# Softmax of a window attention: subtraction and sum moved from six ScalarE instructions to VectorE, beside a long scan

## The chip, the cores and the metric

The kernel runs on one core of a Trainium2 chip. The metric is the device time of one execution in microseconds (us). The engines are named as in the profile: PE (TensorE; PEld are its weight loads), DVE (VectorE), ACT (ScalarE), POOL (GpSimd) and SP (SyncE, which issues most DMAs).

## The reference, cut to what matters

The network has four layers on images of 56 x 56 pixels and 192 channels, eight images. L0, L1 and L2 are state space layers: each runs a selective scan in four directions over all 3136 pixels. L0 has convolutions beside its scan. L3 is a window attention with an MLP. The change touches the softmax of L3 alone:

```python
qkv = xw @ qkv_w.T + qkv_b            # windows of 7 x 7 = 49 pixels, 6 heads
attn = einsum('bhnd,bhmd->bhnm', qn, kn) * scale
attn = attn + (14.0 * sigmoid(rpb))[None]
attn = attn + mask
attn = softmax(attn, axis=-1)         # exp(a - max a) / sum over 49 columns
out = einsum('bhnm,bhmd->bnhd', attn, v)
```

and the scan that runs beside it is, for each direction, channel and state:

```python
h = exp(d_t * A) * h + (d_t * u_t) * b_t
y = einsum('bkdn,bkn->bkd', h, c_t)
```

## The kernel before, in words

**The scan sets the order.** `run` (line 816) cuts the three scan layers of all eight images into units, and each unit into 24 steps, so that there are 9216 steps. One step handles 128 rows (32 channels by 4 states) and 784 pixels. For step s:

- `make` (line 1044) lets ACT write the decay `exp(A*delta)` into a PSUM tile `ps_x`, of which there are two buffers, and lets POOL write `db`, the product of the spread input and B, of which there are four.
- One step later DVE runs the scan over `ps_x` and `db` (line 888), in place in `ps_x`, and multiplies the result with C into `hc`. In every fourth step the scan writes to `hc` instead, and POOL makes the product there.
- Two steps later ACT copies the last column of the scan into `state` (line 876), for the next unit. In the program this copy stands ahead of the next decay on ACT.
- Four steps later PE sums the products of three steps into `ps_y`.

`prepare` (line 980) makes the step sizes of every half unit (12 steps): PE multiplies, ACT loads the softplus table, makes `delta` and loads the table of exp and ln again, POOL makes `du`, and DMAs spread both to 128 rows.

**Everything else is put between the steps.** The convolutions of L0, the norms and the attention of L3 are Python generators. After each step, `run` lets pieces of them go (line 913) for as long as the planned PE and ACT time of the step is not spent. `Meter` (line 92) books a planned cost for each instruction; what is booked for DVE and POOL holds nothing back. `yield 0` ends a piece within a step, `yield 1` asks for a later step. The order of instructions on every engine is thus fixed when the program is built. `in_order` (line 940) keeps it.

**The attention.** `attention_block` (line 1092) handles the image before the one being scanned: images 0 to 6 go beside the scans of the images after them, and image 7 comes when the scans are over, with `self.ending` set and eight PSUM banks instead of two. Each image has eight rows of windows and each row four calls of `pair` (line 1205), two of which run in turn. One call handles two windows: PE puts bias and scores of all six heads into one bank (128 rows by 6 x 49 = 294 columns), DVE takes the maxima `mx` (negated), the exponentials `s` and their sums `sm` are made, DVE inverts the sums, POOL scales `s`, PE transposes it, and so on to the values. There are 7 x 8 x 4 = 224 calls beside the scans and 32 in the ending.

Two forms of the softmax stand in the code. Beside the scans (lines 1244 to 1252) ACT makes six exponentials of 49 columns from the bank, each with a bias from `mx` and an accumulated sum. In the ending (lines 1235 to 1242) DVE adds `mx` to all 294 columns, ACT makes one exponential, and DVE sums.

Of the kernel before, what the change touches and what calls it, by code (L numbers as in the profile page):

```python
# [32 lines left out]
AF = mybir.ActivationFunctionType  # L33
ALU = mybir.AluOpType
AX = mybir.AxisListType
# [23 lines left out]
WT = WS * WS  # L59
BT = NW * WT  # L60
HEADS = 6
# [77 lines left out]
class Net:  # L139
# [1004 lines left out]
    def attention(self, x, wi, bias, wqkv, wpr, q1, q2, stored):  # L1144

        nc = self.nc
# [58 lines left out]
        def pair(w0):  # L1205


            s = q2.tile([128, HEADS, WT], F32, name="s")
            mx = q2.tile([128, HEADS], F32, name="mx")
            sm = q2.tile([128, HEADS], F32, name="sm")  # L1210
            held = yield from self.bank()
            p = held[:, : HEADS * WT]
            for d in range(2):
                nc.tensor.matmul(
                    p[64 * d : 64 * d + 64], self.ident[:WT, :64],
                    bias[:, int(w0 + d == NW - 1)].rearrange("n h m -> n (h m)"),
                    start=True, stop=False,
                )
            for h in range(HEADS):
                for d in range(2):  # L1220
                    at = (h * NW + w0 + d) * WT
                    n = min(64, 6 * BT - at)
                    nc.tensor.matmul(
                        p[64 * d : 64 * d + n, h * WT : (h + 1) * WT], qn[:, at : at + n],
                        win(kn[:, h // 3], w0 + d), start=False, stop=h == HEADS - 1,
                    )
                if h == 2:
                    yield 0
            yield LAG + 1
            nc.vector.reduce_max(  # L1230
                mx, p.rearrange("n (h m) -> n h m", h=HEADS), axis=AX.X, negate=True
            )
            yield 1
            if self.ending:
                nc.vector.tensor_add(
                    s, p.rearrange("n (h m) -> n h m", h=HEADS),
                    mx.unsqueeze(2).to_broadcast([128, HEADS, WT]),
                )
                self.free(held)
                nc.scalar.activation(s, s, AF.Exp)  # L1240
                yield 1
                nc.vector.reduce_sum(sm, s, axis=AX.X)
            else:
                for h in range(HEADS):
                    nc.scalar.activation(
                        s[:, h, :], p[:, h * WT : (h + 1) * WT], AF.Exp,
                        bias=mx[:, h : h + 1], accum_out=sm[:, h : h + 1],
                    )
                    if h % 2:
                        yield 0  # L1250
                self.free(held)
                yield 1
            nc.vector.reciprocal(sm, sm)
            held = yield from self.bank()
            p = held[:WT, : 2 * C].rearrange("n (d e) -> n d e", d=2)
            for d in range(2):
                w = w0 + d
                for c in range(2):
                    nc.tensor.matmul(
                        p[:, d], xw[:, c, w * WT : (w + 1) * WT], wqkv[:, c, 2 * C :],  # L1260
                        start=c == 0, stop=c == 1,
                    )
            nc.gpsimd.tensor_mul(s, s, sm.unsqueeze(2).to_broadcast([128, HEADS, WT]))
            yield LAG
            vt = q2.tile([WT, 2, C], F32, name="vt")
            self.copied(vt, p)
            self.free(held)
            pts = q2.tile([WT, HEADS, 2 * WT], F32, name="pt")
            both = self.ident.rearrange("p (d n) -> p d n", d=2)[:, :, :WT]
            for c in range(2):  # L1270
                held = yield from self.bank()
                p = held[:WT, : 6 * WT].rearrange("m (h d n) -> m h d n", h=3, d=2)
                for h in range(3):
                    nc.tensor.matmul(p[:, h], s[:, 3 * c + h, :], both, start=True, stop=True)
                yield LAG
                self.copied(
                    pts[:, 3 * c : 3 * c + 3, :], held[:WT, : 6 * WT].rearrange("m (h n) -> m h n", h=3)
                )
                self.free(held)
                yield 0  # L1280
            yield 1
            held = yield from self.bank()
            p = held[:CH, : 4 * WT].rearrange("e (c n) -> e c n", c=2)
            for c in range(2):
                for d in range(2):
                    for h in range(3):
                        g = 3 * c + h
                        nc.tensor.matmul(
                            p[HD * h : HD * h + HD, c, d * WT : (d + 1) * WT],
                            vt[:, d, HD * g : HD * g + HD], pts[:, g, d * WT : (d + 1) * WT],  # L1290
                            start=True, stop=True,
                        )
            yield LAG


            for c in range(2):
                nc.scalar.activation(
                    xw[:, c, w0 * WT : (w0 + 2) * WT], p[:, c], AF.Identity, bias=self.v("vb", c)
                )
            self.free(held)  # L1300

        yield from self.together(2, [pair(w) for w in range(0, NW, 2)])

        o = q1.tile([CH, 2, BT], F32, name="ao", tag="kn")
# [258 lines left out]
```

## Time and profile before

| what | us |
|---|---|
| median of three runs (26607.50 to 26614.08) | 26609.99 |
| the profiled execution, its own time | 26624.15 |
| its span in the profile | 26622.0 |
| first scan step to last scan step | 181 to 26060 |
| the ending (attention and MLP of the last image) | 26060 to 26622 |

| engine | busy us | share of the span | instructions |
|---|---|---|---|
| DVE | 24146.0 | 91% | 19164 |
| POOL | 23082.9 | 87% | 13255 |
| PE | 18403.8 | 69% | 76788 |
| ACT | 17059.2 | 64% | 30413 |

Nearly every instruction bears line 109, that of the `Meter` helper, so groups are told apart by their tiles: `ps_x<-dsp,A` is the decay, `ps_x<-ps_x,state,db` a scan, `s<-ps_p,mx` an exponential of the softmax beside the scans, `s<-s` one in the ending, `ps_p` and `ps_t` are PSUM banks. A group's row gives its count, its busy time, the mean of one in ns, and the idle time of the engine before it with what ended it. DVE's instructions overlap at their edges: the next one often starts some 80 ns ahead of the recorded end of the last.

### The profile page before, as it was taken

How to read it: one execution, taken by the hardware profiler on the slowest of the kernel's cores; microseconds unless marked ns; L12 is line 12 of the kernel's file. 1: busy time of each engine (PE TensorE's matmuls, PEld its weight loads, DVE VectorE, ACT ScalarE, POOL GpSimd, SP SyncE). 2: the span in 40 equal slices, each digit the busy share in tenths (PEclk: the TensorE clock that was granted, in tenths of full speed). 3: DMA queues.
4: the chain of work that ended last, by engine and by line, in shares of the span. 5: the costliest groups of instructions: out<-in, count | busy, mean ns of one | idle time of the engine just before them, and what ended most of it. 6: DMA issues, size and time to landing. Idle time of an engine off the chain costs nothing. (4 is left out here: it accounts for less than half of the span.)

```text
span 26622.0 us, 260231 instructions
## 1 busy us (share of the span) xinstructions
PE 18403.8 (69%) x76788; PEld 6418.9 (24%) x76788; DVE 24146.0 (91%) x19164; ACT 17059.2 (64%) x30413; POOL 23082.9 (87%) x13255
## 2 busy tenths in 40 slices
PE   6675567776676767767767676677766777677657
PEld 2221122222222222222222222222222222222214
DVE  5999999999999999998999999999899999999994
ACT  4655566666666656666666766667666676666654
POOL 5888988988889888898888988988888888889992
PEclk7776777777777777777777777777777777777767
DMA  4565565556555566555655556555565555655551
GB/s 95 136 140 121 133 138 135 131 128 140 138 133 131 129 140 137 133 130 129 143 134 135 131 130 143 133 131 129 132 142 132 133 129 135 139 133 134 130 131 41
DMA packets 1503447, 3472.21 MB, mean 130 GB/s; under 512 B 310618, under 2 KB 503219, under 8 KB 1502020
## 3 DMA queue, kind: packets, MB, share of 16 engines
q1 hardware_dynamic: 1496452, 3455.15, 56.7%
q8 instruction: 606, 9.93, 0.1%
q0 software_dynamic: 3072, 0.31, 0.1%
q14 instruction: 821, 6.73, 0.1%
q10 hardware_dynamic: 2496, 0.09, 0.0%
HBM read 1457.23 MB, written 147.89 MB: 60 GB/s over the span
## 5 line engine op out<-in xcount | busy, mean ns | idle before, releaser
L109 POOL TENSOR_TENSOR db<-usp,bt 128x784 f32<-128x784 f32 x9216 | 16851.6, 1857 | 118.6 <-DMA usp<-du 71.4
L109 DVE TENSOR_TENSOR_SCAN ps_x<-ps_x,state,db 128x784 f32<-128x784 f32 x5184 | 9564.9, 1845 | 623.1 <-ACT state L109 266.7
L109 ACT ACTIVATE ps_x<-dsp,A 128x784 f32<-128x784 f32 x9216 | 8444.0, 917 | 2515.6 <-DVE hc L109 2290.5
L109 PE MATMUL ps_y<-hc,esum 128*32 128x392 f32 x36864 | 6882.9, 639 | 1045.1 <-POOL hc L109 696.0
L109 DVE TENSOR_TENSOR hc<-ps_x,ct 128x784 f32<-128x784 f32 x6912 | 6736.8, 975 | 654.1 <-DVE ps_x L109 11.5
L109 POOL TENSOR_TENSOR hc<-hc,ct 128x784 f32<-128x784 f32 x2304 | 4249.2, 1844 | 2448.1 <-ACT state L109 1901.2
L109 ACT COPY state<-ps_x 128x1 f32<-128x1 f32 x5184 | 823.5, 159 | 4579.7 <-DVE hc L109 4558.4
L109 DVE TENSOR_TENSOR_SCAN hc<-ps_x,state,db 128x784 f32<-128x784 f32 x1728 | 3180.1, 1840 | 230.5 <-ACT state L109 109.6
L109 DVE TENSOR_TENSOR_SCAN ps_x<-ps_x,db 128x784 f32<-128x784 f32 x1728 | 3084.8, 1785 | 275.8 <-ACT state L109 120.0
L109 PEld LDWEIGHTS ps_y<-hc,esum 128*32 128x32 f32 x36864 | 1601.2, 130 | 5928.8 <-issue 3126.8
L109 PE MATMUL ps_y<-act,ident 96*96 96x392 f32 x2304 | 1610.2, 835 | 1694.5 <-ACT act L109 1682.9
L109 PE MATMUL ps_p<-act,act 13*96 13x392 f32 (+1 forms) x3072 | 1502.9, 605 | 969.1 <-ACT s L109 294.9
L109 POOL TENSOR_TENSOR du<-delta,act 96x784 f32<-96x784 f32 x768 | 1566.5, 2040 | 66.4 <-ACT delta L109 63.9
L109 PE MATMUL ps_p<-act,wx 96*88 96x392 f32 (+1 forms) x1536 | 985.4, 778 | 627.0 <-ACT delta L109 313.4
L109 ACT ACT_TABLE_LOAD x896 | 1149.6, 1283 | 29.5 <-PE ps_p L109 13.6
L390 ACT ACT_TABLE_LOAD x897 | 1150.9, 1283 | 15.9
L109 DVE TENSOR_TENSOR_SCAN hc<-ps_x,db 128x784 f32<-128x784 f32 x576 | 1024.7, 1779 | 68.5 <-ACT state L109 35.6
L109 PEld LDWEIGHTS ps_y<-act,ident 96*96 96x96 f32 x2304 | 469.8, 226 | 2520.1 <-ACT act L109 1984.1
L109 PE MATMUL ps_p<-xip,diag 96*96 96x448 f32 x2016 | 864.0, 580 | 104.3 <-ACT delta L109 103.6
L109 ACT COPY act<-ps_y 96x784 f32<-96x784 f32 x768 | 928.0, 1208 | 8.5 <-PE ps_y L109 8.5
L109 PEld LDWEIGHTS ps_p<-act,act 13*96 13x96 f32 (+1 forms) x3072 | 471.1, 180 | 1887.5 <-issue 377.5
L109 ACT COPY state<-hc 128x1 f32<-128x1 f32 x1728 | 325.2, 188 | 866.6 <-DVE hc L109 863.9
(222 smaller groups left out, 18022.9 us busy)
## 6 DMA issues: line engine op xcount, KB each, us to landing
dsp<-delta SPq DMA_DIRECT2D x2304, 392.0 KB
usp<-du SPq DMA_DIRECT2D x2304, 392.0 KB
bt<-bcd SPq DMA_DIRECT2D x1536, 392.0 KB
ct<-bcd SPq DMA_DIRECT2D x1536, 392.0 KB
wf<-in_wf SPq DMA_DIRECT2D x128, 288.0 KB
wf<-wf2d SPq DMA_DIRECT2D x128, 288.0 KB
bcd<-bcx SPq DMA_DIRECT2D x256, 134.8 KB
szd<-sz SPq DMA_DIRECT2D x56, 336.0 KB
```

The source lines that it names most:

```text
L109: return call(out, *args, **k)
L390: self.tc.nc.scalar.preload_act_table_set(LN_EXP)
```

## The change

The branch on `self.ending` in `pair` goes, and every image uses the ending's form.

```diff
             yield 1
-            if self.ending:
-                nc.vector.tensor_add(
-                    s, p.rearrange("n (h m) -> n h m", h=HEADS),
-                    mx.unsqueeze(2).to_broadcast([128, HEADS, WT]),
-                )
-                self.free(held)
-                nc.scalar.activation(s, s, AF.Exp)
-                yield 1
-                nc.vector.reduce_sum(sm, s, axis=AX.X)
-            else:
-                for h in range(HEADS):
-                    nc.scalar.activation(
-                        s[:, h, :], p[:, h * WT : (h + 1) * WT], AF.Exp,
-                        bias=mx[:, h : h + 1], accum_out=sm[:, h : h + 1],
-                    )
-                    if h % 2:
-                        yield 0
-                self.free(held)
-                yield 1
+            nc.vector.tensor_add(
+                s, p.rearrange("n (h m) -> n h m", h=HEADS),
+                mx.unsqueeze(2).to_broadcast([128, HEADS, WT]),
+            )
+            self.free(held)
+            nc.scalar.activation(s, s, AF.Exp)
+            yield 1
+            nc.vector.reduce_sum(sm, s, axis=AX.X)
             nc.vector.reciprocal(sm, sm)
```

Beside the scans each of the 224 calls has one tensor_add and one reduce_sum more on DVE, and one ACT instruction of 294 columns in place of six of 49. The bank is given back behind the tensor_add. The ending is as it was.

## The prediction

> **What bounds the kernel now.** First the table by stage. Its columns after the time are PE, PEld, DVE, ACT and POOL, each busy us (instructions).
>
> ```profile
> 181.00:26060.00 25879.00, 17896.13 (x73560) 6131.07 (x73560) 23946.51 (x18696) 16780.22 (x29873) 22962.06 (x13098) 0.76 0.58 133
> ```
>
> The scan stage is 97% of the span. DVE is busy for 23946.5 of its 25879 us (93%), POOL for 89%, ACT for 65%. So the question is what DVE's remaining 1932 us are. The groups of DVE and the waits of DVE in this stage say it:
>
> ```profile
> L109 DVE TENSOR_TENSOR_SCAN ps_x<-ps_x,state,db 128x784 f32<-128x784 f32 x5184 | 9564.9, 1845 | 623.1 <-ACT state L109 266.7 <-ACT ps_x L109 188.7 <-POOL db L109 133.6
> L109 DVE TENSOR_TENSOR hc<-ps_x,ct 128x784 f32<-128x784 f32 x6912 | 6736.8, 975 | 654.1 <-DVE ps_x L109 11.5 <-PE ps_y L109 3.2 <-issue 3.1
> ...
> L109 DVE TENSOR_REDUCE mx<-ps_p 128x6 f32<-128x294 f32 x224 | 94.2, 451 | 3.6 <-PE ps_p L109 3.4
> ```
>
> ```profile
> DVE ps_x L109 <- ACT state L109: 386.6, 315, 52.5
> DVE ps_x L109 <- ACT ps_x L109: 252.6, 182, 5.7
> DVE ps_x L109 <- POOL db L109: 216.6, 65, 62.6
> DVE hc L109 <- ACT state L109: 145.2, 66, 5.2
> DVE hc L109 <- POOL db L109: 98.0, 112, 6.6
> ...
> DVE hc L109 <- ACT ps_x L109: 52.0, 35, 2.7
> ```
>
> About 0.1 us in front of each `hc` product (654.1 / 6912) is a regular pause behind the scan that it reads. True waits are for ACT, 386.6 + 252.6 + 145.2 + 52.0 = 836 us, and for POOL, 315 us, in some 775 of 9216 steps. In the other steps DVE is hardly ever without work. The scan stage is thus bound by DVE: work added there lengthens it, and work taken from ACT shortens it only where ACT made DVE wait.
>
> **The change: what VectorE gets.** The ending of this same profile runs the new form 32 times, so all its prices are here. The timeline of DVE in it (start, us, what):
>
> ```profile
> 26488.06 0.45 DVE L109 TENSOR_REDUCE mx<-ps_t 128x6 f32<-128x294 f32 x1
> 26488.43 0.45 DVE L109 TENSOR_REDUCE sm<-s 128x6 f32<-128x294 f32 x1
> 26488.91 0.19 DVE L109 RECIPROCAL sm<-sm 128x6 f32<-128x6 f32 x1
> 26489.02 0.42 DVE L109 TENSOR_REDUCE sm<-s 128x6 f32<-128x294 f32 x1
> 26489.47 0.19 DVE L109 RECIPROCAL sm<-sm 128x6 f32<-128x6 f32 x1
> 26489.58 0.42 DVE L109 TENSOR_TENSOR s<-ps_p,mx 128x294 f32<-128x294 f32 x1
> ```
>
> Instructions overlap, so I price each from the end of the one before it to its own end. The first sum ends at 26488.88, 0.37 us after `mx` (26488.51). Its reciprocal reads what it wrote, starts only after it and ends at 26489.10: 0.22. The next sum ends at 26489.44 and the add at 26490.00, each 0.34 behind a reciprocal. Over the ending an add costs 0.37 behind anything else. The reciprocal is there before too, where it waits for nothing on DVE; the timeline below has two of them end 0.15 us behind a scan, 0.08 each. Per call: add 0.37, sum 0.36 (between 0.34 and 0.37), reciprocal 0.22 - 0.08 = 0.14, together 0.87 us. Beside the scans there are 224 calls (the row of `mx`): 224 x 0.87 = **195 us**. None of it lies beside other DVE work.
>
> On this the Trainium skill differs. Its page "VectorE: DVE Perf Modes", section "The DRAIN you can't avoid", says that no next operation starts until the pipe of the last one is empty. The rows above show starts 0.08 us ahead of the recorded end. By that rule full durations would count, and the 195 us would be 210. The same page's "Rules for kernel authors" speaks against the change outright, calling the reduction the slowest operation of the engine and advising to restructure; at 294 columns the rows have it no slower than the add (437 against 440 ns).
>
> **What ScalarE loses.** Per call six exponentials and six reads of the accumulator go, and one exponential of 294 columns (0.449 us in the ending) comes. Two calls mostly run together. The timeline beside such a pair, of ACT and DVE:
>
> ```profile
> 4148.42 0.92 ACT L109 ACTIVATE ps_x<-dsp,A 128x784 f32<-128x784 f32 x1
> ...
> 4148.85 1.85 DVE L109 TENSOR_TENSOR_SCAN ps_x<-ps_x,state,db 128x784 f32<-128x784 f32 x1
> 4149.27 0.28 ACT L109 ACTIVATE s<-ps_p,mx 128x49 f32<-128x49 f32 x1
> ...
> 4151.62 1.84 DVE L109 TENSOR_TENSOR_SCAN hc<-ps_x,state,db 128x784 f32<-128x784 f32 x1
> ...
> 4152.49 0.26 ACT L109 ACTIVATION_READ_ACCUMULATOR s<-ps_p,mx 128x1 f32 x1
> 4152.59 0.22 ACT L109 COPY state<-ps_x 128x1 f32<-128x1 f32 x1
> 4153.38 0.23 DVE L109 RECIPROCAL sm<-sm 128x6 f32<-128x6 f32 x2
> 4153.50 0.92 ACT L109 ACTIVATE ps_x<-dsp,A 128x784 f32<-128x784 f32 x1 [0.69 <-DVE hc L109]
> ...
> 4154.52 1.86 DVE L109 TENSOR_TENSOR_SCAN ps_x<-ps_x,state,db 128x784 f32<-128x784 f32 x1 [0.91 <-ACT state L109]
> ```
>
> Twelve exponentials hold ACT from 4149.27 to 4152.75, 3.48 us or 1.74 a call. ACT idles for a third of the stage, so 224 x (1.74 - 0.45) = 289 us less on it is worth nothing by itself. But here DVE waits 0.91 us, and for a particular reason: the next decay starts at 4153.50, when the scan of 4151.62 has ended, though the other `ps_x` was read out at 4151.71. The long burst put the state copy late, so the program gave the next decay the buffer of the scan just before it rather than the one of two before. Comparing the order and the waits of the two built programs, this "tight" buffer occurs in 157 of 9216 steps before (always behind a fourth step) and in 123 after: 41 go, 40 of them within three steps of a softmax, and 7 are new. In the trace DVE waited 40.6 us in front of the scans of those 41 (0.91 to 1.06 each). **Given back: 41 us; new: 7 x 1 = 7 us.**
>
> In the program after, the sum always stands at least one scan behind its add. The exponentials stand directly behind the decay, and behind them mostly come a state copy and the next decay. This is a new wait: the exponential waits for the add, and the state copy and the next decay are queued behind it. After the second add two exponentials (0.9), the copy (0.2) and the decay (0.95) need 2.05 us; DVE has a scan and a product to do, 1.76 + 1.07 = 2.83 (medians over the stage, priced from end to end as above). It is covered, and 0.3 us late only if that step is a fourth one (1.76). The sum finds its exponential done 0.9 us after the add, covered by a scan. In the order, POOL's scaling of `s` keeps its lead over DVE (one `db` ahead in 97 calls before, 103 after). Its two inputs now come 0.56 us apart, where they came together; two scalings and a `db` (1.32 + 1.85) exceeded DVE's 2.83, and some of the 28 us that DVE waits for `db` near the softmax may go. I count 10 us.
>
> Behind `self.free` the bank is free earlier, and the booked ACT time falls by 0.35 us a call: side work moves forward a little. PE has slack (69%) and the last attention beside the scans is over near 24800, far ahead of 26060, so no end moves. The ending is untouched.
>
> Sum: 195 - 41 + 7 - 10 = **+151 us**. On the profiled execution's 26624 that makes 26775; it lies 14 above the median of 26610, so I forecast 26760.
>
> **Bounds.** All waits of DVE over 0.15 us in the steps of a softmax and the four after sum to 98 us in the trace (64 for ACT, 28 for POOL). If all go, +97; with some 20 more for moved side work the time is 26690. If nothing is given back and the waits merely move, +195. If instructions overlapped less beside the scans than in the ending, full durations would count (means: add 0.440, sum 0.437, the pause behind it 0.034, and 0.191 in place of 0.165 for the reciprocal: 0.94 a call), 210. With the POOL waits near the softmax doubled (28), too, it is about +240: 26850.
>
> **Rivals.**
> - *Nothing comes back.* The new wait of ACT for DVE replaces the burst. For it: ACT is in order, and the add stands behind product and scan. Against: 2.05 us are covered by 2.83. Time 26800 to 26850.
> - *Faster: ACT was the hidden bound of the attention.* DVE waits 836 us for ACT in the scan stage. If the shorter softmax spared 30% of them (250 us), the time would be 26610 + 195 - 250 = 26555. It decides from 195 + 53 = 248 us. Against: only 64 us of these waits lie within four steps of a softmax, the rate of waits there is no higher (138 ns a step, 143 elsewhere), and 116 tight buffers, which carry 325 us, are the same in both programs.
> - *In between.* Moved side work spares 142 to 248 us: within 53 us of 26610.
>
> **Chances.** What a measurement of this kernel can tell from no change is about 0.2%, 53 us. Forecast (26720 to 26800) 0.60; nothing back (to 26850) 0.22; more back, still slower (26663 to 26720) 0.09; within 0.2% 0.05; faster 0.03; above 26850 0.01. So slower 0.92, same 0.05, faster 0.03. The range 26690 to 26850 takes in both bounds.
>
> **What would show it.** In the profile after: `s<-ps_p,mx` on DVE and `sm<-s`, 224 each beside the scans, at some 0.44 us; DVE busy about 195 us more in the scan stage; its waits for `ACT state` and `ACT ps_x` some 35 to 60 us less; ACT busy about 290 us less. The ending stays at 562 us. It would be wrong if the waits for ACT fell by hundreds of us, or those for `db` rose.

## The result and the profile after

The changed kernel takes 26789.5 us (median of four runs, 26786.17 to 26803.98), the kernel before 26608.75 (four runs, 26603.94 to 26614.08). The ratio is 1.0069, with an interval of 1.0057 to 1.0082: 152 to 218 us slower, 181 by the medians. The forecast was 150 us more (26760, range 26690 to 26850).

The profiled execution took 26786.89 us, 163 more than that of before (26624.15). The table by stage of the kernel after has the scan stage at 26040 us, where it was 25879:

```profile
181.00:26221.00 26040.00, 17841.40 (x73560) 6120.31 (x73560) 24137.98 (x19144) 16485.24 (x27409) 22962.39 (x13099) 0.76 0.58 132
```

DVE (third engine column) is busy 191.5 us longer, ACT (fourth) 295.0 us less, POOL the same. 161 us of the 163 are in this stage, the rest in the ending, whose code did not change (564.9 after the last scan; 562.1 before). The groups of DVE and ACT in this stage show the new work:

```profile
L109 DVE TENSOR_REDUCE sm<-s 128x6 f32<-128x294 f32 x224 | 97.2, 434 | 0.0
...
L109 DVE TENSOR_TENSOR s<-ps_p,mx 128x294 f32<-128x294 f32 x224 | 94.0, 454 | 0.0
...
L109 DVE RECIPROCAL sm<-sm 128x6 f32<-128x6 f32 x224 | 42.9, 192 | 7.7
```

```profile
L109 ACT ACTIVATE s<-s 128x294 f32<-128x294 f32 x224 | 93.4, 448 | 341.7 <-DVE s L109 340.7 <-POOL db L109 0.8 <-issue 0.2
```

The second row has the add at 454 ns, the first the sum at 434, both with no idle time before them: the sum never waits for its exponential. The reciprocal has its 34 ns pause (7.7 / 224). ACT's new wait for the add is the 341 us in the last row. It delays nothing that DVE needs at the place that the prediction took its example from, as the timeline of the changed kernel shows there (start, us, what; PE and POOL left out):

```profile
4148.26 0.97 DVE L109 TENSOR_TENSOR hc<-ps_x,ct 128x784 f32<-128x784 f32 x1
4149.15 0.82 DVE L109 TENSOR_TENSOR s<-ps_p,mx 128x294 f32<-128x294 f32 x2
4149.64 0.82 ACT L109 ACTIVATE s<-s 128x294 f32<-128x294 f32 x2 [2.77 <-DVE s L109]
...
4149.89 1.84 DVE L109 TENSOR_TENSOR_SCAN hc<-ps_x,state,db 128x784 f32<-128x784 f32 x1
4150.37 0.14 ACT L109 COPY state<-ps_x 128x1 f32<-128x1 f32 x1
4150.54 0.92 ACT L109 ACTIVATE ps_x<-dsp,A 128x784 f32<-128x784 f32 x1
4151.65 0.43 DVE L109 TENSOR_REDUCE sm<-s 128x6 f32<-128x294 f32 x1
...
4152.12 0.19 DVE L109 RECIPROCAL sm<-sm 128x6 f32<-128x6 f32 x1
4152.23 0.42 DVE L109 TENSOR_REDUCE sm<-s 128x6 f32<-128x294 f32 x1
4152.68 0.19 DVE L109 RECIPROCAL sm<-sm 128x6 f32<-128x6 f32 x1
4152.79 1.83 DVE L109 TENSOR_TENSOR_SCAN ps_x<-ps_x,state,db 128x784 f32<-128x784 f32 x1
```

The next decay starts at 4150.54, beside the scan, and is ready at 4151.46; the scan that needs it follows the reciprocal at 4152.79 without the 0.91 us of idle time that stood there. But up to that scan DVE now has 0.74 us of adds and 1.14 of sums and reciprocals to do, where the two reciprocals took 0.15 us before. The waits of DVE in the scan stage after:

```profile
DVE ps_x L109 <- ACT state L109: 349.9, 269, 53.6
DVE ps_x L109 <- ACT ps_x L109: 236.7, 179, 5.8
DVE ps_x L109 <- POOL db L109: 211.8, 70, 62.9
DVE hc L109 <- ACT state L109: 147.3, 66, 5.0
DVE hc L109 <- POOL db L109: 103.4, 99, 6.7
DVE hc L109 <- ACT ps_x L109: 52.2, 33, 2.7
```

For ACT they sum to 786 us (836 before), for POOL to 315 (315 before; both with the 63 us wait of the very first scan, which lies before the stage). Behind them stands one more wait for ACT that grew, that of DVE's instruction on `act` for an ACT instruction on `ps_p`: 32.3 us, 15.2 before. So work was added to the engine that bounds, and 50 us of the waits of its scans and products for the relieved engine went.

### The profile page after: what moved, and what is told of

It reads as the page before. It is cut to its first block, busy times and chain, and to the rows that moved or that the text cites. A ratio compares the mean times of both kernels' runs of the same rounds, so it can differ in the third digit from the quotient of the medians.

```text
span 26785.1 us, 258094 instructions
## 1 busy us (share of the span) xinstructions
PE 18349.7 (69%) x76788; PEld 6408.5 (24%) x76788; DVE 24337.6 (91%) x19612; ACT 16764.6 (63%) x27949; POOL 23082.6 (86%) x13255
```

## The experiments

Two books are kept of each run's trace: the time from the first scan to the end of the last, and what part of it DVE was idle, short pauses included. The rest is DVE's work. The pause of 0.034 us behind a sum, which the price of a reciprocal includes, is idle time here (7.7 us in 224 calls). All times are us; "over before" is by medians, against runs of the kernel before on the same chip. Executions of the kernel before ranged from 26572 to 26640 over the sets of runs.

| run | time | over before | ratio, interval | scan stage | idle | work |
|---|---|---|---|---|---|---|
| before | 26608.75 | | | 25879 | 1932 | 23947 |
| the change | 26789.5 | +181 | 1.0069, 1.0057 to 1.0082 | 26039 | 1901 | 24138 |
| e1_dve_only | 26834.43 | +224 | 1.0082, 1.0069 to 1.0096 | 26103 | 1957 | 24146 |
| e2_act_only | 26625.99 | +16 | 1.0005, 0.9996 to 1.0014 | 25882 | 1933 | 23949 |
| e3_no_max | 26560.22 | -50 | 0.998, 0.9971 to 0.9989 | 25832 | 1964 | 23867 |
| e4_sum_only | 26721.38 | +111 | 1.004, 1.0027 to 1.0052 | 25988 | 1934 | 24054 |
| e5_before_alt | 26545.19 | -59 | 0.9978, 0.9969 to 0.9987 | 25814 | 1864 | 23950 |
| e6_after_alt | 26728.56 | +124 | 1.0046, 1.0034 to 1.0059 | 26000 | 1868 | 24132 |
| e8_one_table | 27226.01 | +622 | 1.0233, 1.0219 to 1.0247 | 26494 | 2559 | 23936 |
| e9_after_one_table | 27348.48 | +744 | 1.028, 1.0266 to 1.0294 | 26615 | 2500 | 24115 |
| e7_alt_no_max | 26462.08 | -152 | 0.9944, 0.9932 to 0.9957 | 25731 | 1866 | 23865 |
| e13_held_booked | 26474.81 | -140 | 0.9947, 0.9935 to 0.996 | 25734 | 1822 | 23912 |
| e14_twice | 26964.71 | +350 | 1.0132, 1.0116 to 1.0147 | 26242 | 1922 | 24320 |
| e15_all | 26285.19 | -336 | 0.9873, 0.9857 to 0.989 | 25553 | 1733 | 23819 |

### The added work without the relief

```diff
             else:
+                sd = q2.tile([128, HEADS, WT], F32, name="sd")
+                nc.vector.tensor_add(sd, p.rearrange("n (h m) -> n h m", h=HEADS),
+                    mx.unsqueeze(2).to_broadcast([128, HEADS, WT]))
                 for h in range(HEADS):
...
                 yield 1
+                nc.vector.reduce_sum(sm, s, axis=AX.X)
             nc.vector.reciprocal(sm, sm)
```

> The kernel before, with the added VectorE work and without the relief of ScalarE: beside the scans each call makes the tensor_add into a scratch tile that nobody reads, and after the six exponentials (which stay as they were) VectorE sums once more. Theory (VectorE bounds the scan stage, each instruction costs its time from end to end, and the relief of ScalarE gave back some 40 us): 224 x (0.37 + 0.35 + 0.14) = 194 us over before, and up to 13 us for 13 more tight buffers in the program (170 against 157): 26800 to 26820. Rival (the relief gave nothing, and a part of the added work is hidden in waits): as the changed kernel, 26770 to 26790. Second rival (the work costs far more than its price, and the relief gave that back): over 26850.

Measured: 26834, +224 (184 to 255 by the interval), just above the theory's range. The work rose by 199 us and the idle time by 25, of which 8 are the reciprocals' pauses (194 by the price, pauses included). The waits of this run have an entry that neither kernel has, since here the sum stands behind the long burst of six exponentials:

```profile
DVE sm L109 <- ACT s L109: 17.3, 18, 1.0
```

So the work costs its price and no less: the first rival falls. The second (over 26850) does too, by 16 us, though the upper end of the interval reaches beyond it.

### The relief without the added work

```diff
+            nc.vector.reduce_max(mx[:, :1], p, axis=AX.X, negate=True)   # in place of six maxima
...
+                nc.scalar.activation(s.rearrange("n h m -> n (h m)"), p, AF.Exp,
+                    bias=mx[:, :1], accum_out=sm[:, :1])                # in place of six
...
+                nc.vector.reciprocal(sm[:, :1], sm[:, :1])
```

> The relief of ScalarE without the VectorE work: VectorE takes one maximum over all 294 columns (as long as the six it replaces), ScalarE makes one exponential of 294 columns with that bias and accumulates one sum for all heads, and VectorE inverts one column. It leaves out the sums of the single heads, so it divides by the sum over six heads. Theory: what the relief is worth, 33 tight buffers of 1 us less (124 against 157) and some further waits near the softmax: 35 to 70 us less than before, 26540 to 26575. Rival (no relief): 26600 to 26615. Second rival (ScalarE was the hidden bound of the attention): 200 us or more less, under 26410.

Measured: 26626, +16, with an interval of -11 to +37 us. The theory fails here and the first rival holds as far as the interval tells: alone, the relief is worth nothing that can be measured. The trace says in part where it went. In the steps that have a softmax in the kernel before and the four after each, DVE's waits fell as expected, from 98 to 63 us, and the 41 tight buffers that the program loses lost all of their 40.6 us. But everywhere else the idle time rose by some 36, and the total stayed (1932, 1933). Going by steps, 15 of the 40.6 us come back exactly three steps behind the lost tight buffer, and 19 us within eight steps as waits for POOL's `db`. The same happens in the changed kernel, 9 and 13 us. Where the rest came back was not followed. One of these places, in the kernel before (timeline of DVE, and of POOL below it):

```profile
24292.48 1.79 DVE L109 TENSOR_TENSOR_SCAN hc<-ps_x,db 128x784 f32<-128x784 f32 x1 [0.51 <-POOL db L109]
24295.33 1.80 DVE L109 TENSOR_TENSOR_SCAN ps_x<-ps_x,db 128x784 f32<-128x784 f32 x1 [1.05 <-ACT state L109]
...
24303.78 1.79 DVE L109 TENSOR_TENSOR_SCAN hc<-ps_x,db 128x784 f32<-128x784 f32 x1
```

```profile
24296.02 1.89 POOL L109 TENSOR_TENSOR hc<-hc,ct 128x784 f32<-128x784 f32 x1
...
24301.87 5.49 POOL L109 TENSOR_TENSOR db<-usp,bt 128x784 f32<-128x784 f32 x3
```

and in the changed kernel, DVE first and POOL after it:

```profile
24443.58 1.79 DVE L109 TENSOR_TENSOR_SCAN hc<-ps_x,db 128x784 f32<-128x784 f32 x1
24445.41 1.80 DVE L109 TENSOR_TENSOR_SCAN ps_x<-ps_x,db 128x784 f32<-128x784 f32 x1
...
24454.88 1.79 DVE L109 TENSOR_TENSOR_SCAN hc<-ps_x,db 128x784 f32<-128x784 f32 x1 [0.86 <-POOL db L109]
```

```profile
24447.16 1.84 POOL L109 TENSOR_TENSOR hc<-hc,ct 128x784 f32<-128x784 f32 x1
24448.97 1.86 POOL L109 TENSOR_TENSOR db<-usp,bt 128x784 f32<-128x784 f32 x1
24450.80 2.23 POOL L109 TENSOR_TENSOR du<-delta,act 96x784 f32<-96x784 f32 x1
24453.00 5.44 POOL L109 TENSOR_TENSOR db<-usp,bt 128x784 f32<-128x784 f32 x3
```

The wait of 1.05 us behind the fourth step's scan is gone, and 0.86 us appear three steps on: POOL works without a pause there, `du` stands in its queue, and the `db` that DVE needs (the first of the last row) is not earlier than it was: it starts 9.42 us behind the first scan shown, 9.39 before. DVE only reaches it sooner.

### Without the maximum, and with half of the change

```diff
-            nc.vector.reduce_max(mx, p.rearrange("n (h m) -> n h m", h=HEADS), axis=AX.X, negate=True)
...
                     nc.scalar.activation(
                         s[:, h, :], p[:, h * WT : (h + 1) * WT], AF.Exp,
-                        bias=mx[:, h : h + 1], accum_out=sm[:, h : h + 1],
+                        accum_out=sm[:, h : h + 1],
```

(beside the scans alone; the ending keeps its maximum)

> The kernel before without the maximum: VectorE's reduction over the scores goes beside the scans, and the six exponentials take no bias (a softmax is the same without it as long as no exponential overflows; with a cosine times 10 plus at most 14 no score of these inputs is above 24). Theory: 224 x 0.37 = 83 us of VectorE less, and 22 tight buffers fewer (135 against 157): 80 to 110 us less than before, 26500 to 26530. Rival (VectorE's work is partly hidden in waits, so that taking it away is worth less than it costs): 30 to 60 us less, 26550 to 26580.

Measured: 26560, -50 (-29 to -77): inside the rival's range, and the interval ends 3 us short of the theory's 80. The work fell by 80 us, near its price (83), but the idle time rose by 32. The 22 tight buffers gave 23 us, and 41 us of other waits came, 13 of them for `db` three steps behind a lost tight buffer. The last of these sections has the same edit where it is worth its full price.

```diff
+                nc.scalar.activation(s.rearrange("n h m -> n (h m)"), p, AF.Exp, bias=mx[:, :1])
...
+                nc.vector.reduce_sum(sm, s, axis=AX.X)
```

> Half of the change: VectorE takes one maximum over all 294 columns, ScalarE subtracts it as the bias of one exponential of 294 columns, and VectorE sums by head. So the tensor_add is spared and the sum stays. Theory: 224 x (0.35 + 0.14) = 110 us more on VectorE, 35 to 70 us back as in the run with the relief alone: 26650 to 26685. Rival (no relief): 26710 to 26725.

Measured: 26721, +111 (+72 to +138): the rival's number, and the theory's upper end (+75) lies inside the interval. The work rose by 107 us, and the idle time is that of before (1934): some 60 us less in waits near the softmax, some 55 more elsewhere and 8 of the reciprocals' pauses. With the run of the relief alone this says that the relief nets about nothing here, while the price of the VectorE work is paid in full.

### Fixed ps_x buffers

```diff
-            t = self.psum.tile([128, 1024], F32, name=f"ps_{tag}", tag=tag)
+            t = self.xs[0]          # a deque of two tiles
+            self.xs.rotate()
```

> The kernel before with two fixed ps_x buffers used in turn, so that the decay of a step never takes the buffer of the scan just before it (1 tight step in the program in place of 157, in front of which VectorE waited 366 us). Theory A (a tight buffer costs about 0.9 us each and that time is gained when it goes): 157 x 0.9 = 140 us less than before, some 26470. Theory B, formed after the first four runs (a wait spared at one step is mostly met again at a later one, since ScalarE and GpSimd stay behind): 0 to 50 us less, 26560 to 26610.

> The changed kernel with the same two fixed buffers. No tight buffer can be spared by the change here, so what lies between this and the kernel before with fixed buffers is the price of the VectorE work and what else the relief of ScalarE is worth. Theory A and B: 190 to 200 us over the kernel before with fixed buffers (the end-to-end price of 193.5), so some 26660 by A and 26750 to 26800 by B. Rival (the relief of ScalarE is worth 40 us without any tight buffers): 150 us over it.

Measured: 26545, -59 (-35 to -82), and 26729, +124 (+90 to +157). For the first, theory B is the nearer one and 9 us beyond its range; A's 140 fails. One of the 157 steps is the very first, whose 62.6 us lie before the stage. In the trace the other 156 lost 98 of the 303 us in front of their scans, and the next eight steps gave 29 back. Of what stays, 167 us stand in front of 26 scans, each over 1.5 us, and did not change with the buffer. Between the two kernels with fixed buffers lie 183 us, 7 under the range that both theories gave and near the price of 194; the time of the second is 21 us under theory B's. Where no tight buffer can be spared the change costs its price less 11 us; the rival of 150 is not met.

### Softplus without table loads, and what a lighter ScalarE is worth

```diff
-        yield from self.table_time()
         for q in range(2):
-            nc.scalar.activation(delta[...], ps[q][:CH, :HC], AF.Softplus)
+            nc.scalar.activation(ps[q][:CH, :HC], ps[q][:CH, :HC], AF.Exp)
+        for q in range(2):
+            nc.scalar.activation(delta[...], ps[q][:CH, :HC], AF.Ln, bias=1.0)
             self.free(ps[q])
-        self.use_ln_exp()
-        self.load["ACT"] += 1.3
```

> The kernel before with the softplus of prepare made of Exp and Ln (both in the table that is loaded anyway), in place of two table loads and a softplus: ScalarE does 2 x 1.283 + 2 x 0.488 = 3.54 us of work in one piece 768 times before, and four instructions of some 0.47 us = 1.9 us now. Theory C (VectorE's 838 us of waits for ScalarE in the scan stage come from these pieces, and not from the softmax): the waits for ScalarE fall by half or more, 300 to 600 us less than before, 26000 to 26300. Rival (they are met again as waits for GpSimd or at other steps): 0 to 100 us less, 26510 to 26610.

> The changed kernel with the same softplus of Exp and Ln. Theory (the price of the VectorE work does not depend on ScalarE's load): 190 to 200 us over the kernel before with that softplus. Rival (a lighter ScalarE leaves nothing for the relief to give back, or more VectorE time is idle and hides the work): less than 150 us over it, or more than 220.

Measured: 27226, +622 (+583 to +657), and 27348, +744. Both expectations of the first fail. ACT has 1472 us less to do (15587.3 busy) and the kernel is 2.3% slower. Without `table_time` the step sizes are made at another step of each half unit, and POOL's `du` comes elsewhere in POOL's queue: behind the second `db` of the half unit in 484 of 768 cases, where it stood behind the third in 684. The waits of DVE in this run, up to 25900 us (its last scan ends at 26676):

```profile
DVE ps_x L109 <- POOL db L109: 578.8, 458, 62.9
DVE hc L109 <- ACT state L109: 362.7, 77, 11.6
DVE ps_x L109 <- ACT state L109: 300.0, 147, 53.4
```

The wait for `db` in the first row was 216.6 us in 65 steps before, and is 578.8 in 458. At the third step of the half units, the one whose `db` now stands behind `du`, waits for `db` grew from 11 to 421 us over the stage. Waits for ACT grew too, from 882 to 1147 us over all of DVE's instructions, though ACT has less to do; why was not followed. The run changed three things at once: the load, the place, and the ACT time that is booked for it (3.6 us a half unit, now 2.0). The next one puts the last two back together, so what each of them cost is not separated. In this kernel, where DVE idles 2559 us, the change costs 122 us and not 190 to 200: the work rose by 180 and the idle time fell by 59. The rival "less than 150" holds: here, with more waiting, more of the added work disappears in it.

Against the run without `table_time`:

```diff
+        yield from self.table_time()       # kept
...
+        self.load["ACT"] += 1.6            # the booked time of before
```

> The kernel before with the softplus of Exp and Ln, but with the place of prepare in the steps (table_time) and the ACT time booked for it kept as they were, so that the side work stays where it was; 768 times ScalarE does 1.9 us of work in place of 3.54. Theory C again (VectorE's waits for ScalarE come from the table loads, and the loss of the run without table_time came from the moved prepare): 100 us or more less than before, under 26500. Rival (a shorter ScalarE is worth nothing by itself, since GpSimd's db is the next to be late): within 50 us of before.

Measured: 26475, -140 (-106 to -173): theory C in its mild form; "within 50 us" fails. With the side work left in place, some 1450 us less of ACT bring 140. DVE's waits for ACT fell from 836 to 750 us, those for POOL rose from 315 to 338:

```profile
DVE ps_x L109 <- ACT state L109: 343.8, 211, 53.0
DVE ps_x L109 <- ACT ps_x L109: 288.5, 205, 5.5
...
DVE hc L109 <- POOL db L109: 114.6, 127, 6.9
DVE hc L109 <- ACT state L109: 90.2, 51, 3.6
...
DVE hc L109 <- ACT ps_x L109: 27.6, 18, 2.4
```

A tenth of what ACT was spared thus reaches the time. The change spares ACT 295 us; by the same share, as an estimate, that would be 30.

### The new work twice, and what adds up

```diff
+                nc.vector.tensor_add(sd, ...)          # a second one, into a scratch tile
...
+                nc.vector.reduce_sum(sm, s, axis=AX.X) # a second one
                 nc.vector.reduce_sum(sm, s, axis=AX.X)
```

> The changed kernel with the new VectorE work beside the scans done twice: a second tensor_add into a scratch tile that nobody reads, and the sum made twice into the same tile. ScalarE's share stays that of the changed kernel (124 tight buffers in the program against 123). Theory (each instruction costs its time from end to end): 224 x (0.37 + 0.35) = 161 us over the changed kernel, up to 185 if the second sum starts only after the first has ended (0.1 us more): 320 to 370 us over the kernel before, 26930 to 26980. Rival (part of the added work hides in waits): under 130 us over the changed kernel.

Measured: 26965, +350, and 175 over the changed kernel (169 when each is taken against its own runs of before): the theory. Twice the work cost twice the price, and the waits did not absorb it (work +182, idle +21 against the changed kernel; 8 of the 21 are the second sum's pause behind the first).

> The kernel before without the maximum beside the scans (as in the run without it) and with two fixed ps_x buffers used in turn. Theory (what VectorE is spared adds to what the buffers gave): 59 us less for the buffers, measured, and 50 to 83 us less for the maximum, measured and by price: 26460 to 26500. Rival (both draw on the same waits, so the sum is less than its parts): 26520 to 26550.

Measured: 26462, -152, the theory. Against fixed buffers alone the missing maximum is worth 83 us, its price (93 when each is taken against its own runs of before), where it gave 50 by itself.

> The kernel before with the three edits that took time off, together: two fixed ps_x buffers used in turn, no maximum beside the scans, and the softplus of Exp and Ln with place and booked time kept. Theory (all three act on VectorE's time or on its waits, and add): 152 us less for the first two and 140 for the third, measured, and up to 40 more since the third alone has 43 more tight buffers than before: 26280 to 26330. Rival (what is left of the waits is GpSimd's, and gains no longer add): 26380 or more.

Measured: 26285, -336 (0.9873, 0.9857 to 0.989), the theory. This version beats both kernels. It holds for these inputs, whose scores stay under 24; with a larger logit scale an exponential without maximum could overflow, which no run here tried.

## Why the prediction held, and which term was off

**What bounds the kernel: right.** The added work lengthened the stage. The runs that add or spare DVE work move with it, and doubling doubles. Work by price (+194 for the change and for the added work alone, +110 for the sum alone, -83 without the maximum) and work by trace (+191, +199, +107, -80) agree within some 5 us, or within 13 when the pauses are counted with the work. How much of it shows in the time depends on the waits around it: 50 of 83 us without the maximum, 122 of 194 in the kernel with the moved side work.

**The prices from the ending: right.** End to end the add takes 0.370 us, the sum 0.350 and the reciprocal 0.226 beside the scans, where 0.37, 0.36 and 0.22 were read off. That is 193.5 us; the trace has 191 us more work and 8 of pauses, together 199 against the 195 of the sum. The full-duration price of 210 is not what the trace has: instructions overlapped beside the scans too. The prediction read the Trainium skill as differing here, and it read too little of it. In the page "VectorE: DVE Perf Modes", the section "The DRAIN you can't avoid" also says that a next operation that is not held starts earlier, and this is what the rows show, with starts 0.08 us ahead of the recorded end. The reduction is no slower than the add in the rows above either, 434 against 454 ns.

**The 41 tight buffers: right in mechanism and in size.** All 41 lost their waits, 40.6 us, in the changed kernel and in both runs with its relief. The 7 new ones have some 3 us more in front of their scans than those steps had before, and not 7.

**What the sum left out: waits that are met again.** In the steps that have a softmax before and the four after each, the waits of DVE fell from 98 to 25 us, more than the 44 that the sum gave back. Elsewhere they rose by 33. The prediction asked what is late next on ACT, and not what is late next on POOL, whose queue does not move when DVE is early. Of these, 14 us are new waits for `db` in front of 22 scans, each three steps behind a lost tight buffer, 0.5 to 0.9 us long and at the same places in image after image; 17 us are the longer wait for ACT before `act`, whose origin was not followed. All told 39 us were given back: 31 less idle time, with 8 of the reciprocals' pauses in it, which the price had paid for already.

**"I count 10 us" for POOL: the named wait went, and as much came elsewhere.** In those steps the waits for `db` fell from 28 to 12 us. The reason given fits the other runs: 8 to 13 us where a sum stands between the two reciprocals and holds the scalings apart (the change, the added work alone, the sum alone, the new work twice), 37 in the run of the relief alone, where none does. But over the stage the waits for `db` stayed as they were, so the term was nothing and not 10.

**Three readings took in the first scan's wait.** The 62.6 us, the longest in the row of `db`, lie before the stage. Without them POOL's waits are 252 us and not 315, the tight buffers that are the same in both programs carry 262 and not 325, and waits away from the softmax come to 136 ns a step and not 143, about as many as near it. The sum uses none of the three.

**The remaining difference.** The sum against the profiled executions was 151, and 163 was measured: 4 more for the work, 5 less given back, 3 in the ending. The other 18 us of the 30 between forecast and median come from the profiled executions, of which that of before lay 15 above the median and that of after 3 below. The ending's 3 us are no effect of the change: with the same code it varied by 24 us between runs.

**The rivals.** "Nothing comes back" came nearer than its 0.22 suggested: 181 by the medians against a price of 194, and alone the relief shows nothing at all. The interval of 152 to 218 us begins at the sum's 151 and holds the bare price too, so the times do not tell the two apart; the 39 us are read from the trace of one execution. The run with the added work alone lies 43 us above the change, which points the same way, but the intervals overlap, and it has 13 tight buffers more. It was not the rival's mechanism, though: the new wait of ACT for the add (341 us in the trace) is covered, as worked out, and part of the spared waits returns through POOL. "ACT was the hidden bound" falls with the relief alone (+16) and with a relief five times as large (-140).

**Open.** Why the relief is worth nothing alone and some 39 us beside the added work was not settled. Of the 41 us of other waits without the maximum, 13 are the ones for `db` three steps behind a lost tight buffer. With fixed buffers they are there already (14 us at the same steps), with the maximum or without, so leaving it out adds none; where the other 28 come from is open. Nor was it shown which part of the far waits in the runs with a short softmax comes from side work that moved forward.

## What to carry to other kernels

In this stage, where one engine is busy for 93% of the time, an instruction moved onto it cost its end-to-end time, read as the distance from the end of the last instruction to its own end; rows of the same instruction elsewhere in the profile gave it to within 3%. What the other engine is spared counts only where a wait for it goes, and each such wait must be followed a few steps on, to the engine that is late next, before it is booked as a gain. A change that moves side work should be tried with its place held too, since the place alone can cost more than the change gives.

## What the runs showed that was not expected

- A kernel with 1472 us less work on ACT was 622 us slower. The work that POOL shares with the scan was made at another step; with place and booked time put back, nearly as light an ACT (1446 us less) gave 140 us.
- The ending, with the same code, took 544 to 568 us after the last scan in the profiled executions.
- One maximum over 294 columns takes DVE as long as six over 49 (453 and 451 ns), so the number of heads is free there, and ACT can subtract the common maximum as a bias. That spares the add and leaves the sum, as the run of half the change shows (+111).
